# Two attentions' scores on TensorE: four parts of 32 rows, or sixteen parts of 32 rows and 32 columns

## The chip, the core and the metric

The kernel runs on one core of a Trainium2 chip. The metric is the device time of one execution in microseconds; the time before is 1734.37 us, the median of three runs (1734.19 to 1734.91). TensorE is the matrix engine, and two of its records are shown apart in the profile: the MATMUL itself (PE) and the load of its stationary operand, the weights (PEld). DVE is VectorE, ACT ScalarE, POOL GpSimd, SP SyncE. All data is float32.

## The reference, cut to what matters

Sixteen sequences of 256 tokens and 256 channels go through a mixture block (a layer norm, an attention over 256 context rows, a router, three experts and a gate) and then through a transformer block: a window self-attention, a cross-attention that keeps the 16 largest scores of each row, and a gated MLP. The change concerns the two score products:

```
scores = jnp.einsum('bnqhd,bnkhd->bnhqk', q, k) / jnp.sqrt(jnp.float32(D))   # self, windows of 128 tokens
attn = jax.nn.softmax(scores, axis=-1)
...
scores = jnp.einsum('bqhd,bkhd->bhqk', q, k) / jnp.sqrt(jnp.float32(D))      # cross, 256 tokens of context
top_s, top_i = jax.lax.top_k(scores, TOPK)
attn = jax.nn.softmax(top_s, axis=-1)
```

There are H = 16 heads of D = 16 channels. The self-attention works in windows of WIN = 128 tokens, two to a sequence; each window gives a 128 x 128 score matrix for each head. The cross-attention gives a 128 x 256 matrix for each head and each half of the tokens.

## The kernel before

**Order of the work.** The program is unrolled. Each sequence passes through eleven stages (`self_keys`, `self`, `cross`, `mlp` and so on), written as Python generators that hand out operations; a planner (`Flow.run`, line 242) picks the next operation among all stages of several sequences by costs written beside them, and emits its instructions. The order on every engine is thus fixed when the program is built, and follows from the written costs, not from what an instruction turns out to take. For TensorE the planner knows two kinds of work: whole (all 128 rows and 128 columns of the array) and tiled, by rows or by columns; it adds `TURN` and `BACK` (lines 136 and 137) when it passes from one kind to the other, and `STAY` and `hold` keep tiled work together.

**Memory.** `banks` (line 384) is a ring of the eight banks of PSUM, each 128 partitions x 512 values; `u` tiles in SBUF are 128 x 512 values. A score burst takes four banks, `sc[0]` to `sc[3]`, at a time.

**How heads lie.** Two heads share a strip of 32 partitions: `W = 2 * D` (line 387), and `rows_of(j)` (line 430) is strip j of four. With two groups c of 128 channels there are 2 x 4 x 2 = 16 heads. The queries `qT` hold [channel, c, token]. The keys are masked (`masked_keys`, line 1268): `kM[c]` holds [channel, a, token] with a = 0 or 1, and for a = 0 the channels of the strip's second head are zero, for a = 1 those of its first. One product of a strip's 32 rows of queries with the keys of both a so gives the scores of both heads.

**The self scores** (`self_attention`, line 1382, its `scores` at 1386, the call at 1392): for each window t, eight multiplications, c = 0, 1 and j = 0 to 3. The stationary operand is 32 rows x 128 tokens of queries, the moving one 32 rows x 256 values (a = 0, 1 and the window's 128 keys). The output is [128 tokens, 256] and goes to half c of bank `sc[j]`. The four strips j use four different parts of 32 rows of the array.

**The cross scores** (`cross_attention`, line 1516, its `scores` at 1521, the call at 1525): for each half t of the tokens and each c, four multiplications j = 0 to 3, with 32 rows x 128 tokens of queries and 32 rows x 512 values (two a, 256 keys), each into all of bank `sc[j]`.

**What follows a burst.** Self: for each j a maximum (DVE, line 1409), four exponentials (ACT, 1418), reciprocals (DVE, 1428), a scaling (POOL, 1433), four transposes on TensorE (1339), a copy (ACT or DVE). Cross: for each j MAX8 and MATCH_REPLACE8 twice (DVE, 1548, 1552, 1583, 1590), exponentials (ACT, 1571), a masked sum (DVE, 1458), a scaling (POOL, 1474) and transposes (1482). Both end in `weigh` (line 1310, the call at 1314): products of the weights with the values, which are tiled by columns: 128 rows x 32 columns, four column parts at a time. The small products at line 1119 have the same form.

Other lines named below: 574 (`by_channel`) and 585 (`by_token`) are the whole-array multiplications of projections, experts and MLP; 744 the products that fold weights at the start.

Of the kernel before, what the change touches and what calls it, by code (L numbers as in the profile page):

```python
# [15 lines left out]
P = 128  # L16
# [4 lines left out]
RH = 512  # L21
H, D = 16, 16
HID = 1024
TAKEN = -(2.0 ** 127)
UNITS = 50

# [25 lines left out]
def t_dve(cols, n=1):  # L52
    return n * (0.07 + cols * 0.00104)
# [254 lines left out]
def pixart_kernel(  # L308
# [9 lines left out]
    nc = tc.nc  # L318
# [3 lines left out]
    def ct(shape, name):  # L322
        return const.tile(shape, F32, tag=name, name=name)
# [39 lines left out]
    wso, wcq, wco = (ct([P, 2, C], n) for n in ("wso", "wcq", "wco"))  # L363
    wm1 = ct([P, 2, 2 * HID], "wm1")
    wm2 = ct([P, HID // P, C], "wm2")

# [63 lines left out]
    def rows_of(j):  # L430

        return slice(W * j, W * (j + 1))
# [16 lines left out]
    def make(*args, **kw):  # L449
        op = Op(*args, **kw)  # L450
        yield op
        return op.out[0] if len(op.out) == 1 else op.out
# [922 lines left out]
    def heads(s, v, ts):  # L1375

        if ts[0] == 0:
            oT = yield from empty()
            s["heads"] = oT, v, []
        return s["heads"]  # L1380

    def self_attention(b, s, ts):
        qT, kM, v = s["self"]
        oT, _, ended = yield from heads(s, v, ts)
        for t in ts:
            def scores(*sc, t=t):


                tok = slice(t * P, (t + 1) * P)
                for c in range(2):  # L1390
                    for j in range(4):
                        nc.tensor.matmul(  # L1392
                            sc[j][:, c, :].rearrange("p (a k) -> p a k", a=2),
                            lhsT=qT.t[rows_of(j), c, tok],
                            rhs=kM[c].t[rows_of(j), :, tok],
                            start=True,
                            stop=True,
                        )
            sc = yield from make(
                PE, 1.07, scores, r=(qT, *kM), new=(banks,) * 4, free=(qT, *kM) if t else (),  # L1400
                tiled="rows", hold=flow.WAIT,
            )
            if t == ts[0]:
                exs = []
                flow.add(self_weigh(ts, v, exs, oT, ended), RANK["self"], KEEP["self"])
            for j in range(4):
                nm = yield from make(
                    DVE, t_dve(512),
                    lambda n, sc=sc, j=j: nc.vector.tensor_reduce(  # L1409
                        n[:, 0:4], heads4(sc[j].t),  # L1410
                        AX.X, ALU.max, negate=True,
                    ),
                    r=(sc[j],), new=(smalls,),
                )

                def exps(u, sc=sc[j], nm=nm):
                    for i in range(4):
                        nc.scalar.activation(  # L1418
                            heads4(u)[:, i, :], heads4(sc.t)[:, i, :], AF.Exp,
                            bias=nm.t[:, i : i + 1], accum_out=nm.t[:, 4 + i : 5 + i],  # L1420
                        )
                ex = yield from make(
                    ACT, t_act(128, 4) + 0.38, exps, r=(sc[j],), w=(nm,), new=(units,),
                    free=(sc[j],), table="exp",
                )
                yield Op(
                    DVE, 0.09,
                    lambda nm=nm: nc.vector.reciprocal(nm.t[:, 8:12], nm.t[:, 4:8]), w=(nm,),  # L1428
                )
                def scale(ex=ex, nm=nm):  # L1430
                    for i in range(4):
                        part = heads4(ex.t)[:, i, :]
                        nc.gpsimd.tensor_scalar(  # L1433
                            part, part, nm.t[:, 8 + i : 9 + i], 1.0, ALU.mult, ALU.mult
                        )
                yield Op(POOL, 1.42, scale, r=(nm,), w=(ex,), free=(nm,), grain=0.355)
                exs.append(ex)
# [10 lines left out]
    def cross_weigh(c, t, v, exs, lefts, oT, ended):  # L1448

        pTs = []  # L1450
        for j in range(4):
# [3 lines left out]
            def mask_out(s, j=j):  # L1455
                left, ex = lefts[j].t, exs[j].t
                for a in range(2):
                    nc.vector.scalar_tensor_tensor(  # L1458
                        ex[:, a, :], left[:, a, :], TAKEN, ex[:, a, :], ALU.is_equal, ALU.mult,
                        accum_out=s[:, a : a + 1],  # L1460
# [55 lines left out]
    def cross_attention(b, s, ts):  # L1516
        (kM, v), qT = s["keys"], s["q", ts]
        oT, _, ended = yield from heads(s, v, ts)
        rounds = [(t, c) for t in ts for c in range(2)]
        for n, (t, c) in enumerate(rounds):  # L1520
            def scores(*sc, t=t, c=c):


                for j in range(4):
                    nc.tensor.matmul(  # L1525
                        sc[j],
                        lhsT=qT.t[rows_of(j), c, t * P : (t + 1) * P],
                        rhs=kM[c].t[rows_of(j), :, :],
                        start=True,
                        stop=True,  # L1530
                    )
            last = n == len(rounds) - 1
            sc = yield from make(
                PE, 1.07, scores, r=(qT, *kM), new=(banks,) * 4,
                free=(qT,) * last + tuple(kM) * (last and t == NT - 1),
                tiled="rows", hold=flow.WAIT,
            )
            exs, lefts, m8s = [], [], []
            flow.add(
                cross_weigh(c, t, v, exs, lefts, oT, ended), RANK["cross"], KEEP["cross"]  # L1540
            )
            firsts = []
            for j in range(4):


                def top(m8, sc=sc[j]):
                    for a in range(2):
                        nc.vector.max(m8[:, 16 * a : 16 * a + 8], sc.t[:, a, :])  # L1548

                def take(*_, j=j, sc=sc[j], firsts=firsts, m8s=m8s):  # L1550
                    for a in range(2):
                        nc.vector.match_replace(  # L1552
                            firsts[j].t[:, a, :], m8s[j].t[:, 16 * a : 16 * a + 8],
                            sc.t[:, a, :], TAKEN,
                        )
                m8s.append((yield from make(DVE, 0.67, top, r=(sc[j],), new=(smalls,))))
                op = Op(DVE, 0.74, take, r=(sc[j], m8s[j]), new=(units,))
                firsts.append(op.out[0])
                yield op
                nm = yield from make(  # L1560
                    POOL, 0.2,
                    lambda n, j=j, m8s=m8s: nc.gpsimd.tensor_scalar(  # L1562
                        n[:, 0:2], m8s[j].t.rearrange("p (a i) -> p a i", a=2)[:, :, 0],
                        -1.0, 1.0, ALU.mult, ALU.mult,
                    ),
                    r=(m8s[j],), new=(smalls,),
                )

                def exps(u, sc=sc[j], nm=nm):
                    for a in range(2):  # L1570
                        nc.scalar.activation(  # L1571
                            u[:, a, :], sc.t[:, a, :], AF.Exp, bias=nm.t[:, a : a + 1]
                        )
                ex = yield from make(
                    ACT, t_act(256, 2), exps, r=(sc[j], nm), new=(units,), free=(nm, sc[j]),
                    table="exp",
                )
                exs.append(ex)
            for j in range(4):

                def top(j=j, firsts=firsts, m8s=m8s):
                    for a in range(2):
                        nc.vector.max(  # L1583
                            m8s[j].t[:, 16 * a + 8 : 16 * a + 16], firsts[j].t[:, a, :]
                        )

                def take(j=j, firsts=firsts, m8s=m8s):
                    for a in range(2):
                        left = firsts[j].t[:, a, :]
                        nc.vector.match_replace(  # L1590
                            left, m8s[j].t[:, 16 * a + 8 : 16 * a + 16], left, TAKEN
                        )
                yield Op(DVE, 0.67, top, r=(firsts[j],), w=(m8s[j],))
                yield Op(DVE, 0.74, take, r=(m8s[j],), w=(firsts[j],), free=(m8s[j],))
                lefts.append(firsts[j])
# [7 lines left out]
    def mlp(b, s, ts):  # L1603
        xb, hT = s["x"], s["m", ts]
        NH = HID // P
        us = []
        for r in range(0, NH, 2):
# [5 lines left out]
            pb = yield from by_channel(  # L1613
                wm1, (hT,), 2, HID + r * P, free=(hT,) if r == NH - 2 else (), ts=ts
            )
# [130 lines left out]
```

## Time and profile before

| | before |
|---|---|
| median of 3 runs | 1734.37 us (1734.19 to 1734.91) |
| the profiled execution's own time | 1736.43 us |
| its span, first to last instruction | 1734.4 us |
| granted TensorE clock, mean | 1.000 |
| MATMUL records, all lines | 12105 |
| line 1392 (self scores) | 512 MATMUL records, 36.7 us busy, mean 400 ns |
| line 1525 (cross scores) | 512 MATMUL records, 74.3 us busy, mean 640 ns |
| line 1314 (products with the values) | 3072 MATMUL records, 99.6 us busy, mean 275 ns |
| lines 574 and 585, whole array | the largest groups: 1536 records of 381 ns, 768 of 381 ns |
| instruction queue (q8) | 96 packets, 1.57 MB |

The span is the time from the first to the last instruction of the profiled execution; the run's own time also holds what lies around it. A float32 multiplication stands in the trace as two pairs of records, each a weight load and a MATMUL (a transpose as one pair). MATMULs are pipelined: a record lasts from its start to its modelled end, and neighbouring records overlap, so the distance between starts says more about cost than the duration. Busy time is the union of the records.

In the chain of waits the profiler goes back from the last instruction, at each step to what released it; the share of a line there says how much of the span its work was the last thing waited for. A stretch view gives the busy time of each engine between two times; a timeline lists merged groups by start and length; the row of a line gives minimum, median and maximum duration of its records.

### The profile page before, as it was taken

The page shows a single profiled execution, that of the slowest core. Times are in us where ns is not written, and L with a number is a line of the kernel's source. Part 1 is how long each engine was busy: PE and PEld are TensorE (multiplying, and loading weights), DVE is VectorE, ACT ScalarE, POOL GpSimd, SP SyncE. Part 2 cuts the span into 40 slices and gives each one's busy share as a digit, 9 for nine tenths or more (in the row PEclk, how much of TensorE's full clock was granted, in tenths as well). Part 3 has the DMA queues.
Part 4 walks back from the last instruction along what each step waited for, and adds up shares of the span by engine and source line. Part 5 has one row for each costly group of instructions (what it writes and reads, how often), then busy time and mean ns, then how long its engine had stood idle before and what let it go on. Part 6 is the DMA issues. An engine that isn't in the chain of part 4 may idle for free.

```text
span 1734.4 us, 36914 instructions
## 1 busy us (share of the span) xinstructions
PE 1712.2 (99%) x12105; PEld 1416.5 (82%) x12105; DVE 1442.5 (83%) x5698; ACT 1150.2 (66%) x2956; POOL 810.4 (47%) x1803
## 2 busy tenths in 40 slices
PE   8999999999999999999999999999999999999999
PEld 6788888788888888788888888888888887888888
DVE  3206598989889979988998989989898999899952
ACT  3316768786767758677768666686877587766632
POOL 1204634564453725554464636573456454633431
PEclk9999999999999999999999999999999999999999
DMA  8400000000000000000000001000000000100101
GB/s 288 149 1 7 7 13 25 2 26 1 15 24 19 8 17 22 1 26 7 15 18 13 20 2 37 8 26 2 26 7 14 7 14 8 38 26 8 32 25 37
DMA packets 33802, 45.12 MB, mean 26 GB/s; under 512 B 5609, under 2 KB 23579, under 8 KB 33099
## 3 DMA queue, kind: packets, MB, share of 16 engines
q1 hardware_dynamic: 33531, 42.70, 7.9%
q8 instruction: 96, 1.57, 0.4%
q14 instruction: 95, 0.78, 0.1%
q10 hardware_dynamic: 80, 0.07, 0.0%
HBM read 38.46 MB, written 4.30 MB: 25 GB/s over the span
## 4 chain that ended last, share of the span: by engine, by line
PE 71%; DVE 18%; ACT 4%; POOL 3%; issue 2%; DMA 0%; SPq 0%; DVEq 0%; ACTq 0%; POOLq 0%
PE bank L574 33%; PE bank L585 19%; PE bank L1482 5%; PE bank L1314 4%; DVE u L1552 3%; DVE u L1458 3%; DVE small L1583 3%; DVE u L1590 3%; DVE small L1548 2%; PE bank L1525 2%; PE bank L1339 2%; PE bank L502 2%; PE bank L1392 1%; PE bank L744 1%; ACT u L1418 1%
## 5 line engine op out<-in xcount | busy, mean ns | idle before, releaser
L1474 POOL TENSOR_SCALAR u<-u,small 128x256 f32<-128x256 f32 x512 | 268.4, 540 | 262.9 <-DVE small L1467 215.6
L574 PE MATMUL bank<-u,w 128*128 128x256 f32 x1536 | 357.8, 381 | 0.4 <-ACT u L1418 0.2
L574 PEld LDWEIGHTS bank<-u,w 128*128 128x128 f32 x1536 | 285.0, 190 | 43.5 <-issue 6.1
L536 ACT COPY u<-bank 128x512 f32<-128x512 f32 x363 | 206.5, 604 | 130.8 <-PE bank L1482 72.1
L1571 ACT ACTIVATE u<-bank,small 128x256 f32<-128x256 f32 x512 | 215.2, 482 | 103.2 <-DVE u L1552 47.5
L574 PE MATMUL bank<-u,wm 128*128 128x256 f32 (+1 forms) x1088 | 243.6, 369 | 0.0
L1433 POOL TENSOR_SCALAR u<-u,small 128x128 f32<-128x128 f32 x512 | 184.2, 383 | 72.7 <-DVE small L1428 64.4
L1548 DVE MAX8 small<-bank 128x8 f32<-128x256 f32 x512 | 190.1, 415 | 29.1 <-PE bank L1525 29.1
L574 PEld LDWEIGHTS bank<-u,wm 128*128 128x128 f32 x1088 | 190.4, 190 | 27.4 <-issue 6.2
L1552 DVE MATCH_REPLACE8 u<-small,bank 128x256 f32<-128x256 f32 x512 | 207.3, 411 | 0.0
L1458 DVE SCALAR_TENSOR_TENSOR u<-u,u 128x256 f32<-128x256 f32 x512 | 207.1, 442 | 0.0
L1590 DVE MATCH_REPLACE8 u<-small,u 128x256 f32<-128x256 f32 x512 | 204.7, 407 | 0.0
L1418 ACT ACTIVATE u<-bank,small 128x128 f32<-128x128 f32 x512 | 182.0, 396 | 15.7 <-DVE small L1409 14.4
L1583 DVE MAX8 small<-u 128x8 f32<-128x256 f32 x512 | 187.1, 410 | 0.0
L585 PE MATMUL bank<-w,u 128*128 128x256 f32 x768 | 182.9, 381 | 1.1 <-DVE u L538 0.6
L585 PEld LDWEIGHTS bank<-w,u 128*128 128x128 f32 x768 | 142.3, 190 | 22.3 <-issue 2.7
L1562 POOL TENSOR_SCALAR small<-small 128x2 f32<-128x2 f32 x256 | 55.3, 218 | 198.3 <-DVE small L1548 135.2
L1482 PE MATMUL bank<-ident,u 128*128 128x128 f32 x1024 | 143.8, 275 | 3.7 <-POOL u L1474 1.5
L1482 PEld LDWEIGHTS bank<-ident,u 128*128 128x128 f32 x1024 | 119.2, 141 | 29.6 <-POOL u L1474 11.0
L1418 ACT ACTIVATION_READ_ACCUMULATOR u<-bank,small 128x1 f32 x512 | 119.8, 234 | 0.0
L516 ACT ACTIVATE u<-bank,eb 128x256 f32<-128x256 f32 x192 | 79.4, 473 | 59.7 <-PE bank L574 40.5
L516 ACT ACT_TABLE_LOAD x89 | 114.2, 1283 | 3.4 <-PE bank L574 1.4
(174 smaller groups left out, 3070.2 us busy)
## 6 DMA issues: line engine op xcount, KB each, us to landing
u<-gates_d SPq DMA_DIRECT2D x51, 256.0 KB
u<-in_ctx_dram SPq DMA_DIRECT2D x16, 256.0 KB
w<-in_L_xcond_e_w_dram SPq DMA_DIRECT2D x3, 1024.0 KB
wada<-in_L_xcond_w_ada_dram SPq DMA_DIRECT2D x1, 2304.0 KB
u<-in_x_dram SPq DMA_DIRECT2D x16, 128.0 KB
u<-in_x_dram SPq DMA_DIRECT2D x32, 64.0 KB
wm<-in_L_xcond_w_m_dram SPq DMA_DIRECT2D x1, 2048.0 KB
out_dram<-u SPq DMA_DIRECT2D x16, 128.0 KB
```

The source lines that it names most:

```text
L536: ACT, t_copy(512), lambda u: nc.scalar.copy(u, pt.t),
L574: nc.tensor.matmul(to[:, c, cols(ts)], lhsT=w[:, k, col + c * P : col + (c + 1) * P], rhs=rhs[k // 2].t[:, k % 2, cols(ts)], start=start, ...
L585: nc.tensor.matmul(to[:, t, :], lhsT=lhs[k // 2].t[:, k % 2, t * P : (t + 1) * P], rhs=w(k), start=start, stop=stop,)
L1418: nc.scalar.activation(heads4(u)[:, i, :], heads4(sc.t)[:, i, :], AF.Exp, bias=nm.t[:, i : i + 1], accum_out=nm.t[:, 4 + i : 5 + i],)
L1458: nc.vector.scalar_tensor_tensor(ex[:, a, :], left[:, a, :], TAKEN, ex[:, a, :], ALU.is_equal, ALU.mult, accum_out=s[:, a : a + 1],)
L1474: nc.gpsimd.tensor_scalar(ex, ex, sm.t[:, 2 + a : 3 + a], 1.0, ALU.mult, ALU.mult)
L1482: nc.tensor.transpose(heads4(pt)[:, 2 * a + k, :], exs[j].t[:, a, k * P : (k + 1) * P], ident,)
L1548: nc.vector.max(m8[:, 16 * a : 16 * a + 8], sc.t[:, a, :])
L1552: nc.vector.match_replace(firsts[j].t[:, a, :], m8s[j].t[:, 16 * a : 16 * a + 8], sc.t[:, a, :], TAKEN,)
L1571: nc.scalar.activation(u[:, a, :], sc.t[:, a, :], AF.Exp, bias=nm.t[:, a : a + 1])
L1583: nc.vector.max(m8s[j].t[:, 16 * a + 8 : 16 * a + 16], firsts[j].t[:, a, :])
L1590: nc.vector.match_replace(left, m8s[j].t[:, 16 * a + 8 : 16 * a + 16], left, TAKEN)
```

## The change

Each multiplication of the two score products becomes four, one for each block of 32 of the 128 tokens. The stationary operand is then 32 rows x 32 tokens, the moving operand stays as it was, and the output goes to the 32 partitions of the bank that belong to the block. Row strip j and token block `at` together choose one of sixteen parts of the array, each 32 rows x 32 columns. A self burst has 32 multiplications in place of 8, a cross burst 16 in place of 4. The written costs (1.07) and the flags of the operation stay.

```diff
+WQ = 32
...
-                tok = slice(t * P, (t + 1) * P)
                 for c in range(2):
                     for j in range(4):
-                        nc.tensor.matmul(
-                            sc[j][:, c, :].rearrange("p (a k) -> p a k", a=2),
-                            lhsT=qT.t[rows_of(j), c, tok],
-                            rhs=kM[c].t[rows_of(j), :, tok],
-                            start=True,
-                            stop=True,
-                        )
+                        for at in range(0, P, WQ):
+                            nc.tensor.matmul(
+                                sc[j][at : at + WQ, c, :].rearrange("p (a k) -> p a k", a=2),
+                                lhsT=qT.t[rows_of(j), c, t * P + at : t * P + at + WQ],
+                                rhs=kM[c].t[rows_of(j), :, t * P : (t + 1) * P],
+                                start=True,
+                                stop=True,
+                            )
...
                 for j in range(4):
-                    nc.tensor.matmul(
-                        sc[j],
-                        lhsT=qT.t[rows_of(j), c, t * P : (t + 1) * P],
-                        rhs=kM[c].t[rows_of(j), :, :],
-                        start=True,
-                        stop=True,
-                    )
+                    for at in range(0, P, WQ):
+                        nc.tensor.matmul(
+                            sc[j][at : at + WQ],
+                            lhsT=qT.t[rows_of(j), c, t * P + at : t * P + at + WQ],
+                            rhs=kM[c].t[rows_of(j), :, :],
+                            start=True,
+                            stop=True,
+                        )
```

## The prediction

> **What bounds the kernel.** I read the busy shares first, then the chain of waits, then the rows of the three lines that use TensorE in parts.
>
> ```profile
> span 1734.4 us, 36914 instructions
> ...
> PE 1712.2 (99%) x12105; PEld 1416.5 (82%) x12105; DVE 1442.5 (83%) x5698; ACT 1150.2 (66%) x2956; POOL 810.4 (47%) x1803
> ...
> PEclk9999999999999999999999999999999999999999
> ...
> PE 71%; DVE 18%; ACT 4%; POOL 3%; issue 2%; DMA 0%; SPq 0%; DVEq 0%; ACTq 0%; POOLq 0%
> PE bank L574 33%; PE bank L585 19%; PE bank L1482 5%; PE bank L1314 4%; DVE u L1552 3%; DVE u L1458 3%; DVE small L1583 3%; DVE u L1590 3%; DVE small L1548 2%; PE bank L1525 2%; PE bank L1339 2%; PE bank L502 2%; PE bank L1392 1%; PE bank L744 1%; ACT u L1418 1%
> ```
>
> TensorE is busy 99% of the span at the full granted clock, and it carries 71% of the chain. A longer score burst is therefore paid, and a shorter one is a gain. The two score lines hold 2% and 1% of the chain, 52 us of 1734; all their bursts together are 64 x 1.07 + 32 x 1.08 = 103 us. So between half of a change in them (the chain's share) and all of it (TensorE's 99%) reaches the end.
>
> The price of a burst is in its rounds. Here is one self-attention burst (16 records), cut into its four rounds; the columns are the stretch, its length, and TensorE's busy time:
>
> ```profile
> 749.19:749.51 0.32, 0.32 (x4) 0.31 (x8) 1.00 0.00 0
> 749.51:749.73 0.22, 0.22 (x8) 0.20 (x4) 1.00 0.00 0
> 749.73:749.95 0.22, 0.22 (x9) 0.20 (x4) 1.00 0.00 0
> 749.95:750.27 0.32, 0.32 (x8) 0.00 (x0) 1.00 0.00 0
> ```
>
> Each multiplication in the code leaves two pairs of records, a weight load and a MATMUL each: 16 sequences x 2 tiles x 8 = 256 calls and 512 records on line 1392. Four parts run side by side, so 16 records need four rounds of 0.216 us. The first round is longer by 0.10 us (its weights have nothing to hide behind), the last by 0.09 us (the array empties before the next mode of tiling starts). The next view has the durations, minimum/median/maximum, of these records, and below them the lines that use four column parts with 32-wide weights:
>
> ```profile
> L1392 PEld LDWEIGHTS bank<-u,u x512: 181/184/185, 155.5 to 1501.9; 32*128 32x128 f32 x171
> L1392 PE MATMUL bank<-u,u x512: 374/374/478, 155.5 to 1502.1; 32*128 32x256 f32 x171
> ...
> L1525 PE MATMUL bank<-u,u x512: 587/640/692, 205.9 to 1652.0; 32*128 32x512 f32 x171
> ...
> L1314 PEld LDWEIGHTS bank<-u,v x3072: 106/110/110, 179.0 to 1678.6; 128*32 128x32 f32 x192
> L1314 PE MATMUL bank<-u,v x3072: 272/273/297, 179.0 to 1678.7; 128*32 128x128 f32 x192
> ...
> L1119 PE MATMUL bank<-u,rw x128: 379/379/403, 71.3 to 1346.9; 128*32 128x256 f32 x128
> ```
>
> A MATMUL that opens a burst is long by its wait for weights: 478 - 374 = 104 ns and 692 - 587 = 105 ns with 128-wide weights, 297 - 273 = 24 ns and 403 - 379 = 24 ns with 32-wide ones. Last, the first four MATMULs of the same burst, and a cross burst between two column bursts (start, length):
>
> ```profile
> 749.20 0.50 PE L1392 MATMUL bank<-u,u 32*128 32x256 f32 x4
> ...
> 1414.22 1.14 PE L1525 MATMUL bank<-u,u 32*128 32x512 f32 x8
> 1415.29 1.08 PE L1314 MATMUL bank<-u,v 128*32 128x128 f32 x32
> ```
>
> Four of 478 ns end within 0.50 us: their starts lie 20 ns apart in all, 6.7 ns for each part.
>
> **The change, part by part.** *Streamed columns: nothing.* A block of 32 tokens still streams all 256 (self) or 512 (cross) columns. Before, 16 records on 4 parts made four rounds; after, 64 records on 16 parts make four rounds of the same 0.216 us. Cross: 8 records on 4, then 32 on 16, two rounds of 0.43 us both times. The words "sixteen in place of four" hold four times as many instructions, not a quarter of the time.
>
> *Weights of the first round: a gain.* 104 - 24 = 80 ns a burst. The two 24s are from 128-row weights; that 32 rows cost the same with 32 columns I take from 184 against 190 ns at 128 columns. 96 bursts x 80 ns = 7.7 us less.
>
> *Starting sixteen parts: a loss.* At 6.7 ns each the last part starts 15 x 6.7 = 100 ns after the first, not 3 x 6.7 = 20, and it ends that much later: 80 ns a burst, 7.7 us more. No row has sixteen parts. Bounds: nothing, if a spacing hides; above, records that start only as densely as in the column burst, (1.08 - 0.27)/31 = 26 ns a pair. I take 6.7 ns, since it stands on row parts and column parts alike.
>
> *Emptying the array: nothing.* The last round's 0.09 us is the same after row parts (here) and after column parts: L1314 before the next line takes 1.08 us with its last record's 0.27 in it, and the following work starts 0.20 us after that record's start, 0.107 of stream and the same 0.09.
>
> *More instructions.* 32 bursts x 24 more calls and 64 x 12 make 1536 calls, 6144 records beside 24,210. Their supply: the instruction queue moves 1.57 MB in 96 packets now and needs 6144 x 64 B = 0.39 MB, 24 packets, more, on DMA engines that stand at 0 to 10% after the start. The sequencer must hand out 16 pairs in 216 ns, 6.75 ns an instruction. Its rate shows in the trace's records of TensorE's semaphore waits: between the end of one and the start of the next lie 74 ns with 8 or 12 matmul instructions between, 88 with 16, 117 with 24. That is 3.6 ns an instruction, and one or four semaphores waited for among them make no difference. It stands up to 16 to 18 weight loads, some 32 instructions, ahead of the array. A self burst was 32 instructions and fully in hand; now it is 128, so the second eight of the first sixteen blocks come live, 32 x 3.6 = 115 ns against the 100 they need: 15 ns, at most 1.4 us over 96 bursts. Upper bound at the 13 ns an instruction of the column burst: see the first rival.
>
> *Waits.* No bank, semaphore or queue is added. Bank j is now written by four blocks and is complete with the fourth; the blocks of bank 0 start first, so DVE's maximum (line 1409) and MAX8 (line 1548) start when they did. The planner's cost of a burst (1.07) is unchanged, so the order of all engines' work stays.
>
> The sum: 32 and 64 bursts x (-80 + 80) ns = 0, plus 0 to 1.4 us. By rows: 1734.4 to 1735.8. The profiled execution's span is 1734.4 and the runs' median 1734.37, so no correction; I say 1735.
>
> The Trainium skill has two rules against the change. "TensorE: Matmul & The Clock Gate", Part 3, says that MATMULs start strictly in program order and only weight loads are pulled ahead. In program order both passes of a part follow each other, so by it four parts could not start within 20 ns, as they do here; the row decides, but by the rule a self burst would take 33 rounds for 4 and a cross burst 17 for 2, some 600 us more. The same page, Part 1, has starts never closer than about 25 ns. By it 64 records need 1.6 us, 0.74 more than 0.86, or 24 us over 32 self bursts; the 6.7 ns between parts here says it holds for one part, not across parts.
>
> **Rivals.** *Starved blocks (slower).* Place: the second half of each burst, past the 32 instructions in hand. For it: the densest stretch that lasts, the column burst, needs no more than 13 ns an instruction, so nothing longer than 24 instructions shows the 3.6. It decides from 6.75 ns an instruction. At 13 ns: a self burst's other 48 pairs take 48 x 26 = 1.25 us where 0.77 from first to last start was enough, +0.48 x 32 = 15 us; a cross burst's sixteenth block starts 16 x 26 = 0.42 us after the first, not 0.10, +0.32 x 64 = 20 us. Together 36 us, half to all of it paid: 1752 to 1770; at 8 ns, where self fits and cross starts 0.15 us late, 1739 to 1744. Against: the 3.6 ns.
>
> *Not sixteen at a time.* The array may overtake only between row strips, so that the blocks of one strip go in order: the second pass of one starts with the first of the next. Self: 9 rounds of 0.216 for 4, +1.08 us x 32; cross: 5 of 0.43 for 2, +1.29 x 64; together 117 us, less 7.7 for the shorter first load, 1843; TensorE's present waits (gaps between MATMUL starts beyond stream and mode change, 40 us in all from 100 us on) may swallow up to 40 of it, so 1803 to 1843. For it: no row splits both ways. Against: overtaking works in both directions alone.
>
> *The starts are hidden (faster).* If sixteen starts cost no more than four, the 7.7 us remain: 1726.7; with half the spacing 1730.5. Against: 6.7 ns wherever parts are used.
>
> **How the numbers follow.** No change 0.44 (own range 1733 to 1737); starved 0.26; not sixteen 0.10; hidden starts 0.18; slower for a cause not listed 0.02. The time is the likeliest's, 1735. For 8 in 10 the range takes in the faster rival nearly whole and the starved one up to the middle of its prices: 1727 to 1760. What a measurement can tell is about 0.2%, 3.5 us. Faster 0.18, the same 0.44, slower 0.38.
>
> **What would show it.** Right: self bursts of 64 records and cross bursts of 32 keep 1.08 and 1.07 us; MATMULs of both lines have a maximum 24 ns over the minimum; the first sixteen start within 100 ns. Starved: the first four or eight blocks start 6.7 ns apart and later ones further. Not sixteen: bursts of 2 us and more. Hidden: 1.00 us. I am wrong if bursts keep their length and the span still moves by more than 4 us; then a consumer of the banks is what I misjudged.

## The result, and the profile after

The changed kernel takes 1743.13 us (median of four runs, 1742.65 to 1743.96) against 1734.3 us before: a ratio of 1.0049, 95% interval 1.0036 to 1.0061. It is slower by half a per cent, well clear of what a measurement can tell. The profiled execution took 1743.96 us with a span of 1742.0 us, 7.6 more than before. Its page, busy times first, then the instruction queue, then the chain of waits by engine and by line (line 1392 is now 1393, 1525 is 1527, 574 is 575):

```profile
span 1742.0 us, 43112 instructions
...
PE 1721.1 (99%) x15177; PEld 1414.3 (81%) x15177; DVE 1442.7 (83%) x5698; ACT 1149.3 (66%) x2956; POOL 807.4 (46%) x1803
...
q8 instruction: 120, 1.97, 0.5%
...
PE 75%; DVE 17%; POOL 2%; ACT 2%; issue 2%; DMA 1%; SPq 0%; DVEq 0%; POOLq 0%; ACTq 0%
PE bank L575 34%; PE bank L586 19%; PE bank L1483 5%; PE bank L1315 4%; DVE u L1554 3%; PE bank L1340 3%; PE bank L1527 3%; DVE small L1585 2%; DVE small L1550 2%; DVE u L1592 2%; PE bank L1393 2%; DVE u L1459 2%; PE bank L503 2%; PE bank L1109 1%; PE bank L745 1%
```

TensorE's busy time grew by 8.9 us and its share of the chain from 71% to 75%; VectorE, ScalarE and GpSimd did the same work in the same time, within 0.4%. So the loss is on TensorE. The instruction queue moves 24 packets and 0.40 MB more than before. The first self burst has become longer, here in the timeline (start, length) before and after:

```profile
155.49 1.15 PE L1392 MATMUL bank<-u,u 32*128 32x256 f32 x16
...
155.46 1.50 PE L1393 MATMUL bank<-u,u 32*32 32x256 f32 x64
```

Now the rows of the two changed lines (durations minimum/median/maximum):

```profile
L1393 PEld LDWEIGHTS bank<-u,u x2048: 101/104/105, 155.5 to 1509.2; 32*32 32x32 f32 x187
L1393 PE MATMUL bank<-u,u x2048: 374/374/399, 155.5 to 1509.4; 32*32 32x256 f32 x187
...
L1527 PE MATMUL bank<-u,u x2048: 584/588/612, 206.5 to 1659.4; 32*32 32x512 f32 x187
```

The number of records is four times that of before, and a MATMUL that opens a burst is now 399 - 374 = 25 ns longer than the others where it was 104 longer: the shorter first load is there. What the rows can't show is the distance between starts. The next view cuts one self burst (64 records, its first start at 155.459) into four stretches; the columns are the stretch, its length, then the busy time of MATMULs and of weight loads, each with the number of records that touch the stretch:

```profile
155.46:155.70 0.24, 0.24 (x17) 0.23 (x32) 1.00 0.00 0
155.70:156.10 0.40, 0.40 (x33) 0.21 (x2) 1.00 0.00 0
156.10:156.60 0.50, 0.50 (x43) 0.37 (x30) 1.00 0.00 0
156.60:156.88 0.28, 0.28 (x24) 0.00 (x0) 1.00 0.00 0
```

A burst has 64 weight loads. 32 of them start in the first quarter of a microsecond: both passes of the sixteen blocks of channel group c = 0. In the next 0.40 us only two start, both of the 17th call. The other 30 come after 156.10. TensorE counts as busy all the while, since the parts that were fed go on; the loads betray the stop.

Record by record, in ns from the first start: the first MATMULs of the sixteen blocks start at 0 to 100, 6.7 apart; their second passes at 240 to 340; the 17th call (c = 1, first block) at 456, on time; the 18th at 650 where its part had been free since 463; and the following ones 16.7 apart up to 884, with second passes up to 1121. Before, the last start was at 772. All 32 self bursts read 1120 to 1122 ns. The difference of 349 ns is 187 (650 for 463), 14 x (16.7 - 6.7) = 140 and about 21 for a first load that shows once more. A cross burst, by contrast, has its last start at 553 ns, as before (median of 64; ten bursts are longer, at 570 to 1101 ns, and four were before, at 680 to 1168; what they add is 1.0 us in all, 1.3 before).

Summed over the whole trace, the time from the start of each of line 1393's MATMULs to the next start grew by 11.1 us (32 x 0.349 = 11.2). After the lines of the transposes (1340 and 1483), of `by_channel` (575) and of the cross scores (1527) it shrank by 1.2, 0.9, 1.1 and 0.4 us. TensorE's idle time fell by 1.3 us (22.2 to 20.9), so part of this may be shorter waiting for others; the cause isn't shown. 11.1 - 3.6 = 7.5 is nearly what the span lost, 7.6.

### The profile page after: what moved, and what is told of

Read it like the earlier page. It is cut to its first block, busy times and chain, and to the rows that moved or that the text cites. A ratio compares the mean times of both kernels' runs of the same rounds, so it can differ in the third digit from the quotient of the medians.

```text
span 1742.0 us, 43112 instructions
## 1 busy us (share of the span) xinstructions
PE 1721.1 (99%) x15177; PEld 1414.3 (81%) x15177; DVE 1442.7 (83%) x5698; ACT 1149.3 (66%) x2956; POOL 807.4 (46%) x1803
## 4 chain that ended last, share of the span: by engine, by line
PE 75%; DVE 17%; POOL 2%; ACT 2%; issue 2%; DMA 1%; SPq 0%; DVEq 0%; POOLq 0%; ACTq 0%
PE bank L575 34%; PE bank L586 19%; PE bank L1483 5%; PE bank L1315 4%; DVE u L1554 3%; PE bank L1340 3%; PE bank L1527 3%; DVE small L1585 2%; DVE small L1550 2%; DVE u L1592 2%; PE bank L1393 2%; DVE u L1459 2%; PE bank L503 2%; PE bank L1109 1%; PE bank L745 1%
## 5 line engine op out<-in xcount | busy, mean ns | idle before, releaser
L1419 ACT ACTIVATE u<-bank,small 128x128 f32<-128x128 f32 x512 | 181.6, 393 | 15.9 <-DVE small L1410 11.2
```

Source lines behind the costliest of these rows:

```text
L1419: nc.scalar.activation(heads4(u)[:, i, :], heads4(sc.t)[:, i, :], AF.Exp, bias=nm.t[:, i : i + 1], accum_out=nm.t[:, 4 + i : 5 + i],)
```

## Experiments

The theory that the trace after suggests: TensorE's queue takes instructions ahead of the array in program order, some 17 calls of four instructions, and a place in it comes free only when the oldest call has ended. In the self burst the first call's second MATMUL starts at 240 and lasts 374, to 614; the 18th call's load starts at 646. The rivals: every added instruction costs something (8.8 us for 6144); the array must be empty before the 18th call; the instructions are not delivered fast enough. The last has no place for a stop of 190 ns that is followed by calls 16.7 ns apart.

**Cross scores alone in blocks of 32.** The self scores are as before the change:

```diff
-                        for at in range(0, P, WQ):
-                            nc.tensor.matmul(
-                                sc[j][at : at + WQ, c, :]...
+                        nc.tensor.matmul(
+                            sc[j][:, c, :]...
```

> Cross scores in blocks of 32, self scores as before. The queue theory (TensorE's queue takes 17 calls ahead of the oldest unfinished one, and a place comes free only when the oldest call has ended) has no cost here, since a cross burst is 16 calls: 1734.3 us, within 1 us, and cross bursts of 553 ns from first to last start. The rival, that every added instruction costs something (8.8 us for 6144), gives half of it for 3072: 1738.7 us.

Measured: 1736.31 us against 1735.38 us before on the same chip, ratio 1.0008 (0.9999 to 1.0017), and a span of 1734.5 us against 1734.4. Cross bursts have 553 ns from first to last start in the median, and 52 of the 64 have 553 to 555. A cost of 3072 more instructions can't be seen: it is at most 3 us by the interval, and half of 8.8 us lies outside.

**Self scores alone in blocks of 32.** The same, the other way about: line 1527 is undone.

> Self scores in blocks of 32, cross scores as before. Queue theory: the whole loss, 1742 to 1744 us, with self bursts of 1121 ns from first to last start in place of 772. Added instructions: 1738.7 us.

Measured: 1742.52 us against 1735.38, ratio 1.0045 (1.0030 to 1.0061); all self bursts at 1120 ns. The loss is the self burst's: 7.1 us here, and the interval holds the whole 8.8.

**Blocks of 64 tokens in both.** Eight parts, a self burst of 16 calls and 64 instructions:

```diff
-WQ = 32
+WQ = 64
```

> Both scores in blocks of 64 tokens, eight parts of 32 rows and 64 columns. A self burst is 16 calls. Queue theory: no stop inside a burst; the first load costs about 51 ns (64 columns, half of 104) and the starts 7 x 6.7 = 47, together 98 ns against 124 before: first to last start 746 ns for self and 527 for cross, 26 ns less in 96 bursts, 2.5 us less, 1731 to 1733 us. Added instructions (2048 more than before): 1737.2 us.

Measured: 1735.02 us against 1735.38, ratio 0.9998 (0.9989 to 1.0007), span 1733.1. The bursts are what was expected, 745 and 527 ns from first to last start. One self burst in the timeline (start, length), and the row of the line (durations minimum/median/maximum):

```profile
154.95 1.12 PE L1393 MATMUL bank<-u,u 32*64 32x256 f32 x32
...
L1393 PE MATMUL bank<-u,u x1024: 374/374/426, 154.9 to 1500.5; 32*64 32x256 f32 x171
```

1.12 is 745 ns and the last record's 374; 426 - 374 = 52 ns is the wait for a first load of 64 columns. There is no stop. Of the 2.5 us taken from the bursts (2.3 by the starts in the trace) the span shows 1.3 against the first profile, and the timed runs can't tell the kernel from the one before. The expected gain of 2.5 us is thus not shown: 0.4 was measured, with an interval from 1.9 us less to 1.2 more.

**Strip by strip, self scores alone in blocks of 32.** The two channel groups of a strip follow each other, so that the first 16 calls lie on eight parts:

```diff
-                for c in range(2):
-                    for j in range(4):
+                for j in range(4):
+                    for c in range(2):
```

> As the run with self scores alone in blocks of 32, but each strip's two channel groups follow each other, so that the first 17 calls reach nine parts. Queue theory: nine parts start within 60 ns; a few calls (those whose places the first four calls leave) start at 650 to 700 ns, the others only after 1050, since the fifth call, the second on its part, ends there; first to last start about 1850 ns, 1765 to 1772 us. The drain theory (the array must be empty before the 18th call starts) has nothing start between 60 and 980 ns on the other seven parts; first to last about 1880. Added instructions: no difference to the run with self scores alone.

Measured, in one run: 1768.09 us, span 1766.2, 1876 ns from first to last start. The total alone is nearer to the drain theory's, so it has to be read from the starts. One burst (first start 156.865) in stretches, columns as above:

```profile
156.86:157.10 0.24, 0.23 (x8) 0.23 (x17) 1.00 0.00 0
157.10:157.28 0.18, 0.18 (x16) 0.18 (x8) 1.00 0.00 0
157.28:157.50 0.22, 0.22 (x21) 0.21 (x9) 1.00 0.00 0
157.50:157.72 0.21, 0.21 (x25) 0.17 (x7) 1.00 0.00 0
157.72:157.94 0.22, 0.22 (x21) 0.10 (x1) 1.00 0.00 0
```

Eight MATMULs and seventeen loads in the first stretch: eight parts are fed while the other eight stand empty, except for one load of the ninth part. Loads go on starting between 0.64 and 0.86 us, on the tenth to twelfth parts too, while the first eight still run. The array is not empty then, so the drain theory falls. The records give the rule exactly. The 65th instruction is the 17th call's first load: it starts at 128, 29 after the first load's end at 99. The 66th, its MATMUL, starts at 425, 27 after the first MATMUL's end at 398. The 68th, its second MATMUL, starts at 641, 27 after the fourth instruction's end at 614, and the 69th, the next call's load, at 645. In the 32 bursts these four delays are 26 to 29 (one 118), 27 to 28, 26 to 28 and 31 to 32 ns. So there are 64 places, one to an instruction; the place of instruction n goes to n + 64 when n and all before it have ended (by the modelled ends of the records). My 17 calls were these 64 and what the first call had already left. The 17th call's late start I had not foreseen.

**Twice the self scores, in blocks of 64.** Self scores alone, each product made twice into the same place, 128 instructions on eight parts:

```diff
-                for c in range(2):
+                for c in (0, 1, 0, 1):
```

> Self scores alone in blocks of 64 tokens, and every product of the self scores made twice into the same place, so that a burst is 32 calls, 128 instructions, on eight parts. The queue theory, by now exact (64 places in TensorE's queue, each freed in program order when its instruction has ended): the 17th call needs the second MATMUL of the first call at 914 ns at the earliest, and the first call ends at 640, so nothing stops: 745 + 4 x 216 = 1609 ns from first to last start, 1752 to 1763 us. The rival, that a burst of more than 64 instructions stops at the 65th whatever its parts: the 17th or 18th call starts about 1050 ns after the first and the following ones 16.7 ns apart, 1.8 us from first to last start.

Measured, in one run: 1608 ns from first to last start (1609 in some bursts), 1759.73 us. A timeline row shows it as 1.98 us, 1608 ns and a record's 374:

```profile
156.29 1.98 PE L1393 MATMUL bank<-u,u 32*64 32x256 f32 x64
```

So it isn't the 65th instruction that stops, but the 65th that comes before the first ones have ended. On eight parts it is wanted at 914 ns, and its place is free long before. The trace of the first burst shows how near it is: the 22nd to 24th calls' loads start at 738, 755 and 772, 16.7 apart, as instructions that come through freed places do, but are done 128 ns later, before their MATMULs start at 947 to 961.

**Twice the cross scores, in blocks of 32.** Cross scores alone, each product made twice into the same place, sixteen parts and 512 streamed columns:

```diff
+                for _ in range(2):
                     for j in range(4):
                         for at in range(0, P, WQ):
```

> Cross scores alone in blocks of 32 tokens, and every product of the cross scores made twice into the same place: 32 calls on sixteen parts with 512 streamed columns. Queue theory: the first call's second MATMUL starts at 453 and ends 587 later, at 1040 ns; the 17th call starts when its part is free, at 882; the 18th at 1070 to 1075 in place of 889, and the others 16.7 ns apart; first to last start about 1758 ns, 1795 to 1815 us. Without such a queue (the drain of the 17th call onward had another cause, in the self burst alone): 553 + 2 x 429 = 1411 ns and 1775 to 1790 us.

Measured, in one run: 1760 ns from first to last start (median of 64), 1798.71 us. The 17th call starts at 882, the 18th at 1075, the others 16.7 apart. One burst (first start 205.633) in stretches, columns as above:

```profile
205.63:206.08 0.45, 0.45 (x16) 0.23 (x32) 1.00 0.00 0
206.08:206.50 0.42, 0.42 (x32) 0.10 (x1) 1.00 0.00 0
206.50:206.70 0.20, 0.20 (x17) 0.10 (x1) 1.00 0.00 0
206.70:207.20 0.50, 0.50 (x31) 0.37 (x30) 1.00 0.00 0
207.20:207.91 0.71, 0.71 (x31) 0.00 (x0) 1.00 0.00 0
```

32 loads, then one and one, then 30: the picture of the self burst, in a burst that had no stop while it was half as long. With both other stream length and other line, the stop lies where the queue puts it.

**Blocks of 64 and a planner that knows of them.** An attempt at a kernel that beats both:

```diff
-                PE, 1.07, scores,
+                PE, 1.045, scores,
```

(at both places, with WQ = 64)

> Both scores in blocks of 64 tokens, as in the run before, with the cost written for a score burst lowered from 1.07 to 1.045, so that the planner's order fits the shorter burst. Queue theory: bursts of 745 and 527 ns as before; 1731 to 1735 us. If the order of the other work decides more than 26 ns a burst: anything from 1728 to 1742 us.

Measured: 1762.35 us, ratio 1.0160 (1.0146 to 1.0173), above both ranges that were given. The bursts have their 745 and 527 ns (medians). In the trace it is the time from a start to the next after the lines of `by_channel`, of the transposes 1483 and of `by_token` that grew, by 8.3, 8.3 and 4.1 us. 25 ns less in a written cost gives every engine another order. TensorE is idle for 37.9 us of the span where it was idle for 22.2 before, the loads of line 1483 wait 22.2 us for GpSimd's scaling (line 1475) where they waited 11.0, and the granted clock is 0.50 in three stretches of 3.4 us, which is about 5 us of time at most, half of these stretches. These name where the time shows; which step of the order brings it about is open.

## Why the prediction was wrong where it was

*The number.* The measured 1743.1 us lies in the range given for 8 in 10, 1727 to 1760, but above 1733 to 1737, the range of the case that gave the 1735 and had the largest chance. The wide range reached it only because it took in the starved blocks, and the runs show another cause than theirs. That the time falls inside is luck.

*Bounds and streaming.* TensorE as the bound, rounds of 0.216 and 0.43 us, four times the instructions and the same streamed time: right, and so were the 24 packets more of the instruction queue. Of 11.1 us in the bursts 7.5 reached the span, within "half to all".

*First loads and starts.* 24 ns in place of 104, and 15 x 6.7 = 100 in place of 20: both as said (25 and 100). In the cross burst they cancel to the nanosecond, 553 before and after (medians).

*More instructions: the step that failed.* The prediction said that the sequencer stands some 32 instructions ahead, that the rest of a burst comes live at 3.6 ns an instruction, and that this costs 15 ns a burst, 1.4 us in all. Two things in it were off. There were 64 instructions in hand and not 32: what I had counted in the trace before were loads not yet started, in whole-array and column work, and I took the count for the room. So the first sixteen blocks started without the 15 ns in every self burst and in 54 of the 64 cross bursts. And I took a place to be free when its instruction starts. It is free when the instruction has ended, in program order. With sixteen parts the 64 places hold one call for each part and no more, the oldest needs 614 ns to end, and the parts want the next sixteen calls from 456 on. The delivery itself was about right, 16.7 ns a call or 4.2 an instruction. Why no more than 16 to 18 loads stood ahead in the trace before, with 64 places, the runs don't show.

*The rivals.* The starved blocks had the right sign, the right place in the self burst and a near price (0.48 us for 0.35), but not the cause: not the rate but the room. In the cross burst, where it asked 0.32 us, nothing was lost. Sixteen parts do work side by side, in 553 ns, so the second rival falls; the starts are not hidden, so the third does.

*The two rules that were weighed.* The first sixteen MATMULs start before any second pass, and starts of different parts lie 6.7 ns apart. The Trainium skill, "TensorE: Matmul & The Clock Gate", has MATMULs in program order (Part 3, on what overlaps) and starts no closer than 25 ns (Part 1, where it doesn't speak of parts); across parts the runs show neither. The same page's table at its head gives TensorE's queue a depth of 64. The runs agree with that figure and add what the page doesn't have, when a place comes free. The prediction went by its own count of 32 instead.

## What to carry to other kernels

Smaller parts of the array didn't speed up these products, whose stationary operand is already 128 wide; they trade a shorter first load (104, 52 or 24 ns for 128, 64 or 32 columns) against 6.7 ns for each part that starts. Count the instructions from the oldest unfinished call to the one that must start next: with float32, four to a call, 64 places are one call on each of sixteen parts, and both bursts with a second round on them stopped (256 and 512 streamed columns), while eight parts keep two. When an engine is 99% busy, look at the distance between starts and at the weight loads, since a half-fed array looks just as busy.

## What the runs showed of the hardware that was not expected

A place in TensorE's queue is handed on 26 to 32 ns after the modelled end of the instruction 64 before it (128 after 99, 425 after 398, 641 after 614, 646 after 614). Instructions that come through such places arrive 4.2 ns apart (16.7 a call). Calls on different parts overtake each other within the 64, in both directions of tiling at once: sixteen first passes started before any second one.
